# Third context attention: row maxima head by head on the whole TensorE array, its steps interleaved, and two of its four projections ahead of the feed-forward block

## The chip, the cores and the metric

The kernel runs on one core of one Trainium2 chip. The metric is the device time of one execution in microseconds; the text gives it as the median of three runs. TensorE's work appears in the profile under PE (the matmuls) and PEld (the loads of the stationary operand); DVE is VectorE, ACT is ScalarE, POOL is GpSimd and SP issues most DMAs.

## The reference

The program is a network of twelve residual blocks on `x` (4 batches of 128 tokens with 128 channels) with a context of 4 x 2048 rows of 96 values. The change concerns the tenth block, a cross-attention of 8 heads with 16 values each, and by its place the ninth, a feed-forward block with quantized weights. The tenth block, cut to what matters:

```
def _L3_xattn_ref(x, y, Wq, bq, Wk, bk, Wv, bv, Wo, bo):      # x: 4x128x128, y: 4x2048x96
    q, k, v = x @ Wq + bq, y @ Wk + bk, y @ Wv + bv           # 8 heads of 16
...
    weight = jnp.einsum('bhqd,bhkd->bhqk', q, k) * scale
    weight = jax.nn.softmax(weight, axis=-1)                  # over 2048 keys
    out = jnp.einsum('bhqk,bhkd->bhqd', weight, v)
    return out.transpose(0, 2, 1, 3).reshape(B, SQ, D_EMBED) @ Wo + bo
```

The block's input is the layer norm of `x`, and its result is added to `x`. All of it is in 32-bit floating point.

## The kernel before, in words

`program` (line 1847) runs the blocks one after another; each block's function opens its own pools of SBUF and PSUM, and a block's weights are loaded into two alternating buffers by `nxt()` of the block before (the list WEIGHTS, line 1839). Within a block the framework's scheduler may exchange instructions that do not depend on each other, so the order in the code is nearly, but not wholly, the order on an engine.

The ninth block, `bit_ffn` (from line 1678), is a chain on VectorE: two layer norms, a quantization to 8 bits, a small product on TensorE (`h_ps`, line 1738), a Gelu, a third layer norm over 512 columns, a second quantization and a second product (`y_ps`, line 1754). Ahead of that chain TensorE forms a sum over the weights (`tot`, line 1696), from which VectorE derives the weights' scale (`wm`, `wi`) and quantizes them (`qw`, lines 1704 to 1707).

The tenth block is `narrow_attention` (from line 553). Its heads are laid in two sets `s` of four; head `g` of a set lies in partitions 32g to 32g + 31, 16 of them its values, one a row of ones in the keys that carries a bias. After the layer norm the queries of all batches are formed (`q_ps`, line 582). Then come, for each batch `b`:

- `project(b)` (line 598) forms the keys `kT` (8 matmuls of 512 columns, `k_ps`, line 605) and the values `v` (16 matmuls of 136 columns, `v_ps`, line 616) and copies them to SBUF, the copies alternating between ScalarE and VectorE (`self.copy`, lines 318 and 320).
- `maxima(b, s, kT)` (line 625) forms all scores of a set with the queries in the rows (`s_ps`, line 633). The four heads use 32 rows of the array each, so four matmuls of 512 columns run side by side; they write two tiles of two PSUM banks each, and VectorE reduces each tile of 1024 columns to two maxima (`na_m`, line 638). At the end the smallest negated maximum of each head (`nmx`, line 641) is transposed (`m_tr`) and added to the queries (line 645), as the factor of the keys' row of ones.
- `weighted(b, s, ...)` (line 649) takes the keys in four groups of four chunks. For a group it forms the scores with the keys in the rows (`t_ps`, line 657, four heads side by side again), ScalarE takes exponentials (`p`, line 663), and one group later TensorE multiplies with the values (`av`, line 670).
- `finish` (line 679) divides by the sums and multiplies with the output weights (`o_tr`, `on_tr`, `y`).

The loop (lines 705 to 727) first projects batch 0 and takes its first maxima alone. Then a step is one group of `weighted` with one step of the maxima of the next set beside it, and one step of the projection of the next batch as long as there are any. Two PSUM banks stand for each `t_ps`, `s_ps`, `k_ps` and `v_ps` tile: all draw on one pool of three such tiles.

Of the kernel before, what the change touches and what calls it, by code (L numbers as in the profile page):

```python
# [9 lines left out]
F32 = mybir.dt.float32  # L10
# [4 lines left out]
ALU = mybir.AluOpType  # L15
AX = mybir.AxisListType.X
PSUM = bass.MemoryType.PSUM

P = 128
B = 4  # L20
# [250 lines left out]
class Net:  # L271
# [279 lines left out]


    def narrow_attention(self, nxt):

# [3 lines left out]


        nc, tc = self.nc, self.tc  # L560
        wqo, wkv = self.load("qo3"), self.load("kv3")
        scale = 1.0 / math.sqrt(ND)
        with ExitStack() as es:
            one = es.enter_context(tc.tile_pool(name="na1", bufs=1))
            wk = es.enter_context(tc.tile_pool(name="na2", bufs=2))
            pp = es.enter_context(tc.tile_pool(name="na3", bufs=4))
            ps = es.enter_context(tc.tile_pool(name="na_sc", bufs=3, space=PSUM))
            mi = es.enter_context(tc.tile_pool(name="na_mi", bufs=1, space=PSUM))
# [9 lines left out]

            q = one.tile([P, 2, N], F32, name="q")
            mm = ps.tile([P, 2, 512], F32, tag="sc", name="q_ps")  # L580
            for s in range(2):
                nc.tensor.matmul(mm[:, s], wqo[:, s * P : s * P + P], xT, start=True, stop=True)
                nc.vector.tensor_scalar(
                    q[:, s], mm[:, s], self.col("bq3")[:, s : s + 1], scale, ALU.add, ALU.mult)

            nmx = []
# [10 lines left out]

            def project(b):

                kT = wk.tile([P, 2, S], F32, tag="kT", name="kT")  # L600
                v = wk.tile([P, NCH, NH * VW], F32, tag="v", name="v")
                for at in range(0, S, 512):
                    mm = ps.tile([P, 2, 512], F32, tag="sc", name="k_ps")
                    for s in range(2):
                        nc.tensor.matmul(
                            mm[:, s], wkv[:, s * P : s * P + P],
                            self.ctxT[: DC + 1, b * S + at : b * S + at + 512], start=True, stop=True)
                    self.copy(kT[:, :, at : at + 512], mm)
                    yield kT, v
                for c in range(0, NCH, 6):  # L610
                    mm = ps.tile([P, 2, 512], F32, tag="sc", name="v_ps")
                    n = min(6, NCH - c)
                    for j in range(n):
                        at = b * S + (c + j) * P
                        w = NH * VW
                        nc.tensor.matmul(
                            mm[:, j // 3, j % 3 * w : j % 3 * w + w], self.ctxT[: DC + 1, at : at + P],
                            wkv[:, 2 * P : 2 * P + w], start=True, stop=True)
                    for j in range(0, n, 3):
                        k = min(3, n - j)  # L620
                        self.copy(
                            v[:, c + j : c + j + k].rearrange("p c w -> p (c w)"), mm[:, j // 3, : k * w])
                    yield kT, v

            def maxima(b, s, kT):

                qs = q[:, s, b * T : b * T + T]
                part = self.small(16, "na_m")
                for j in range(4):
                    ts = [ps.tile([P, 2, 512], F32, tag="sc", name="s_ps") for _ in range(2)]  # L630
                    for g in (0, 2, 1, 3):
                        lo = g * 32
                        nc.tensor.matmul(  # L633
                            ts[g // 2][:, g % 2], qs[lo : lo + 32], kT[lo : lo + 32, s, j * 512 : j * 512 + 512],
                            start=True, stop=True)
                    for i, t in enumerate(ts):
                        at = j * 4 + i * 2
                        nc.vector.tensor_reduce(part[:, at : at + 2], t, axis=AX, op=ALU.max, negate=True)  # L638
                    yield
                t = nmx[s]  # L640
                nc.vector.tensor_reduce(
                    t[:, ND::32], part.rearrange("p (j g) -> p g j", g=4), axis=AX, op=ALU.min)
                tr = mi.tile([P, B, P], F32, tag="mi", name="m_tr")
                nc.tensor.transpose(tr[:, 0], t, self.ident)
                nc.vector.tensor_add(qs, qs, tr[:, 0])
# [3 lines left out]
            def weighted(b, s, kT, v, av):  # L649

                qs = q[:, s, b * T : b * T + T]
                for c0 in range(0, NCH, 4):
# [13 lines left out]
                    def values(c0=c0, p=p):  # L666
                        for j in range(4):
                            for g in range(4):
# [3 lines left out]
                                    p[g // 2][:, g % 2, j], start=c0 + j == 0, stop=c0 + j == NCH - 1)  # L672

                    while late:
                        late.pop()()
# [23 lines left out]
            def run(*gens):  # L699

                gens = [iter(g) for g in gens if g is not None]
                while gens:
                    gens = [g for g in gens if next(g, gens) is not gens]

            for kv in project(0):
                pass
            run(maxima(0, 0, kv[0]))
            done = None
            for b in range(B):
                av = avp.tile([P, 2, P], F32, tag="av", name="av")  # L710
                more = iter(project(b + 1)) if b + 1 < B else iter(())
                ahead = []
                for s in range(2):
                    if s == 0:
                        top = maxima(b, 1, kv[0])
                    else:
                        top = maxima(b + 1, 0, ahead[0]) if ahead else None
                    for i, _ in enumerate(weighted(b, s, *kv, av)):
                        if done and i == 0:
                            finish(*done)  # L720
                            done = None
                        if top:
                            next(top)
                        ahead = next(more, ahead)
                    run(top)
                done = (b, av)
                kv = ahead
# [950 lines left out]
    def bit_ffn(self, nxt):  # L1678
# [3 lines left out]
        with ExitStack() as es:  # L1682
# [26 lines left out]
            def quantized(x, d, j):  # L1709
# [6 lines left out]
                nc.vector.tensor_scalar_mul(sc, sc, 127.0)  # L1716
                t = one.tile([P, B, d], F32, tag=f"qt{j}", name="qt")
                nc.vector.tensor_mul(t, x, bc_in(sc, d))
# [22 lines left out]
            nc.scalar.activation(self.flat(h), self.flat(h), AF.Gelu)  # L1741
            hn = one.tile([P, B, 512], F32, name="hn")
            self.layernorm(one, h, hn, w=self.row("ln2_g"), b=self.row("ln2_b"), tag="ln2")
            q, sc = quantized(hn, 512, 1)
            qT2 = one.tile([P, B, 4, P], BF16, name="qT2")
# [76 lines left out]
class _Doubled:  # L1822
# [17 lines left out]
    ("l0x",), ("mamba", "dtp"), ("l0f",), ("qk1", "vo1"), ("r7", "r7b"), ("moe1", "moe2"),  # L1840
    ("qk2", "vo2"), ("l2a",), ("l2f",), ("qo3", "kv3"), ("l3a",), ("l3f",),
]
# [4 lines left out]
def program(tc, A, out):  # L1847
    with ExitStack() as es:
        net = Net(es, tc, A)
        for i, (block, args) in enumerate(BLOCKS):  # L1850
# [9 lines left out]
            if i in CTX_TO:  # L1860
                ces.close()
        tc.nc.sync.dma_start(out.rearrange("b t c -> t b c"), net.x)

# [16 lines left out]
```

## Time and profile before

| | us |
|---|---|
| median of three runs | 1784.24 (1782.26 to 1784.53) |
| the profiled execution | 1783.64, span of its instructions 1781.5 |
| TensorE busy, PE (PEld) | 1273.4 (681.7) |
| VectorE, ScalarE, GpSimd busy | 1002.5, 631.2, 139.3 |
| mean granted TensorE clock | 0.801 |

The profile is of one execution, and its times are counted from the first instruction. A row of groups has the source line, the engine, the operation, the tiles written and read, the shapes and a count, then the busy time in us and the mean of one in ns, then the engine's idle time just before these instructions and what ended most of it. A 32-bit matmul appears as two rows of MATMUL and two of LDWEIGHTS, so counts of rows are twice the matmuls'. [...] successive ones overlap in the record, and the distance between their starts is the better price. A timeline row has the start, the time from the first start to the last end of the merged instructions, and in brackets the idle time before. In a table of stretches, each row has the stretch and its length, the busy time of the engines with the number of instructions, then the mean granted clock (1.00 is full speed), the DMA share and GB/s.

### The profile page before, as it was taken

To read this page: it belongs to the slowest core of one execution; us is meant where nothing else is said; L and a number is where in the kernel's file an instruction comes from. 1 tells how busy PE (TensorE), PEld (TensorE's weight loads), DVE (VectorE), ACT (ScalarE), POOL (GpSimd) and SP (SyncE) were. 2 spreads that over 40 slices of the span, in tenths; PEclk is the share of its full clock that TensorE was granted. 3 is DMA by queue.
4 is the path that set the end of the run, shared out by engine and by line. 5 is a ranking of instruction groups with operands and counts; after the bars stand their busy time and mean duration, and the time that the engine had idled before them with its cause. 6 is when DMAs were issued, how large, how long until landed. Compare 5 with 4: busy or idle time off the path is not lost.

```text
span 1781.5 us, 15501 instructions
## 1 busy us (share of the span) xinstructions
PE 1273.4 (71%) x6140; PEld 681.7 (38%) x6140; DVE 1002.5 (56%) x1556; ACT 631.2 (35%) x804; POOL 139.3 (8%) x107
## 2 busy tenths in 40 slices
PE   0367654667689999999946443889866518899867
PEld 0146641222343444444412222664324304554544
DVE  5842345999425676767656875223446674443435
ACT  0642114554315465656434101323422211333342
POOL 2000000446200000000000100000003010000000
PEclk9975555779858999999967766887878656998878
DMA  5000000000400000000001002100000000000010
GB/s 148 0 1 0 1 0 0 0 24 1 134 16 24 1 0 1 1 0 1 1 0 47 0 1 82 37 21 18 0 1 1 8 0 0 2 1 1 6 45 6
DMA packets 9076, 28.18 MB, mean 16 GB/s; under 512 B 1140, under 2 KB 6941, under 8 KB 7717
## 3 DMA queue, kind: packets, MB, share of 16 engines
q1 hardware_dynamic: 7208, 23.70, 4.6%
q10 hardware_dynamic: 1792, 3.45, 0.6%
q8 instruction: 50, 0.82, 0.2%
q14 instruction: 26, 0.21, 0.0%
HBM read 26.88 MB, written 0.26 MB: 15 GB/s over the span
## 4 chain that ended last, share of the span: by engine, by line
PE 62%; DVE 24%; ACT 5%; issue 5%; POOL 3%; DMA 1%; POOLq 0%; ACTq 0%; DVEq 0%
PE av L513 12%; PE sc L487 11%; PE av L933 3%; PE s_ps L633 3%; DVE na_m L638 3%; PE mm L1227 3%; PE t_ps L657 3%; PE q_ps L433 2%; DVE h L1144 2%; PE av L670 2%; PE h_ps L1576 2%; PE st L910 2%; PE y_ps L1583 2%; PE y_ps L1149 1%; POOL hc L1147 1%
## 5 line engine op out<-in xcount | busy, mean ns | idle before, releaser
L513 PE MATMUL av<-s,ctx 128*97 128x512 f32 x448 | 211.0, 629 | 19.4 <-ACT s L511 19.3
L487 PE MATMUL sc<-q_aug,ctxT 99*128 99x512 f32 x448 | 207.5, 607 | 1.8 <-DVE q_aug L434 1.8
L489 ACT COPY s<-sc 128x1024 f32<-128x1024 f32 x112 | 113.0, 1010 | 94.9 <-PE sc L487 94.9
L513 PEld LDWEIGHTS av<-s,ctx 128*97 128x97 f32 x448 | 76.6, 174 | 146.9 <-issue 108.9
L510 DVE TENSOR_TENSOR s<-s,mbs 128x1024 f32<-128x1024 f32 x112 | 128.9, 1219 | 5.0 <-ACT mbs L507 5.0
L638 DVE TENSOR_REDUCE na_m<-s_ps 128x2 f32<-128x1024 f32 x64 | 75.8, 1220 | 90.1 <-PE s_ps L633 89.9
L487 PEld LDWEIGHTS sc<-q_aug,ctxT 99*128 99x128 f32 x448 | 83.7, 195 | 96.3 <-issue 79.0
L511 ACT ACTIVATE s<-s 128x1024 f32<-128x1024 f32 x112 | 113.5, 1053 | 10.8 <-DVE s L510 8.2
L493 DVE TENSOR_TENSOR m<-m,s 128x1024 f32<-128x1024 f32 x72 | 88.0, 1223 | 21.9 <-ACT s L489 20.8
L1149 PE MATMUL y_ps<-hc,consts 128*128 128x512 f32 x128 | 75.1, 722 | 33.7 <-POOL hc L1147 30.8
L663 ACT ACTIVATE p<-t_ps 128x1024 f32<-128x1024 f32 x64 | 62.0, 1021 | 92.8 <-PE t_ps L657 92.8
L1147 POOL TENSOR_TENSOR hc<-h,cs 128x1024 f32<-128x1024 f32 x32 | 77.5, 2432 | 86.1 <-DVE h L1144 85.9
L524 DVE RECIPROCAL rsum<-y 128x2 f32<-128x2 f32 x40 | 6.6, 165 | 133.5 <-PE y L521 133.5
L1144 DVE TENSOR_TENSOR_SCAN h<-dA,dbu 128x512 f32<-128x512 f32 x64 | 74.4, 1204 | 3.7 <-ACT dA L1141 3.5
L933 PE MATMUL av<-kv,p 128*128 128x65 f32 x256 | 56.9, 419 | 19.1 <-ACT p L929 19.1
L336 POOL TENSOR_TENSOR ln_sq<-ln_xc 128x512 f32<-128x512 f32 (+1 forms) x19 | 23.3, 1225 | 552.7 <-DVE ln_xc L334 546.2
L633 PE MATMUL s_ps<-kT,q 32*128 32x512 f32 x256 | 63.5, 709 | 2.1 <-DVE na_m L638 1.1
L933 PEld LDWEIGHTS av<-kv,p 128*128 128x128 f32 x256 | 55.3, 332 | 21.0 <-ACT p L929 15.0
L657 PE MATMUL t_ps<-q,kT 32*128 32x128 f32 x1024 | 56.3, 328 | 8.8 <-DVE na_m L638 5.8
L353 PE MATMUL tr_xnT<-consts,xn 128*128 128x128 f32 x32 | 8.7, 428 | 70.3 <-DVE xn L343 30.2
L1149 PEld LDWEIGHTS y_ps<-hc,consts 128*128 128x128 f32 x128 | 26.0, 223 | 83.2 <-POOL hc L1147 57.0
L657 PEld LDWEIGHTS t_ps<-q,kT 32*128 32x128 f32 x1024 | 46.6, 223 | 27.1 <-DVE na_m L638 16.2
(574 smaller groups left out, 2122.0 us busy)
## 6 DMA issues: line engine op xcount, KB each, us to landing
w_moe<-in_moe SPq DMA_DIRECT2D x2, 2048.0 KB, 8.0
ctxT<-in_ctxT SPq DMA_DIRECT2D x4, 768.0 KB, 12.3
rows<-in_rows ACTq DMA_DIRECT2D x1, 2048.0 KB, 12.1
w_l3f<-in_l3f SPq DMA_DIRECT2D x1, 1920.0 KB, 8.2
w_l0x<-in_l0x SPq DMA_DIRECT2D x1, 1024.0 KB, 5.7
w_l0f<-in_l0f SPq DMA_DIRECT2D x1, 1024.0 KB, 4.9
w_mamba<-in_mamba SPq DMA_DIRECT2D x1, 976.0 KB, 4.7
w_r<-in_r SPq DMA_DIRECT2D x1, 960.0 KB, 5.1
```

Source lines behind the costliest of these rows:

```text
L487: nc.tensor.matmul(sc[:, i], self.ctxT[:, at : at + P], qg, start=True, stop=True)
L489: nc.scalar.copy(s, sc)
L510: nc.vector.tensor_sub(p, p, bc_mid(mbs, 2))
L511: nc.scalar.activation(p, p, AF.Exp)
L513: nc.tensor.matmul(av[: DC + 1], self.ctx[:, b * NCH + chunks[j + i]], p[:, i], start=j + i == 0, stop=j + i == n - 1)
L633: nc.tensor.matmul(ts[g // 2][:, g % 2], qs[lo : lo + 32], kT[lo : lo + 32, s, j * 512 : j * 512 + 512], start=True, stop=True)
L638: nc.vector.tensor_reduce(part[:, at : at + 2], t, axis=AX, op=ALU.max, negate=True)
L657: nc.tensor.matmul(ts[g // 2][:, g % 2, j], kT[g * 32 : g * 32 + 32, s, at : at + P], qs[g * 32 : g * 32 + 32], start=True, stop=True)
L933: nc.tensor.matmul(av[:, 0:65], ts[h][:, c], v[:, b * NCH + 2 * c + h], start=h + c == 0, stop=h == 1 and c == HC - 1)
L1144: nc.vector.tensor_tensor_scan(h[:, half], self.flat(dA), dbu[:, half], 0.0, ALU.mult, ALU.add)
L1147: nc.gpsimd.tensor_mul(hc, h, bc_mid(cs, 2))
L1149: nc.tensor.matmul(y[:, half], self.ident, hc[:, half], start=n == 0, stop=n == 15)
```

## The change

Five edits, all in or around the tenth block:

- A new function `narrow_keys` runs after the eighth block and before `bit_ffn`. It loads the weights of keys and values into a pool of its own and runs the projections of batches 0 and 1; `project` is now a method, works in tiles of one PSUM bank (14 a batch), and has all its copies on ScalarE.
- The queries are also laid out as `qz`: for each set and head a full 128 rows, zero outside of the head's 32. GpSimd writes the zeroes, ScalarE and VectorE copy the heads in.
- `maxima` forms the scores of one head at a time with `qz` on all 128 rows, into tiles of one bank from a pool of two (`sp`), and VectorE reduces each tile of 512 columns on its own. `t_ps` has a pool of two tiles of two banks instead of its share in three. The projections of batches 2 and 3 stay in the loop and draw on `sp` too, all in the first half of the batch before.
- A step of the loop is spread: two head steps of the maxima, the scores of a group, one head step, a projection tile, the product with the values of the group before, one head step, further projection tiles.
- In `bit_ffn` the third layer norm is taken in place, and one temporary shares a buffer.

In the built program the order on TensorE is: `out_ps` of the eighth block, the 48 matmuls of `narrow_keys`, then `tot` and the rest of `bit_ffn`. Within the loop a step without projections reads three `s_ps`, 16 `t_ps`, one `s_ps`, 16 `av`. On VectorE `wm`, `wi` and the quantization of the weights stand after the first quantization of the input instead of before the first layer norm. On GpSimd the zeroing of `qz` stands between the last square of `bit_ffn` and that of this block's layer norm.

```diff
+    def narrow_keys(self, es):
+        pool = es.enter_context(self.tc.tile_pool(name="na_w", bufs=1))
+        self.wkv = pool.tile(list(self.A["kv3"].shape), F32, name="w_kv3")
+        self.nc.sync.dma_start(self.wkv, self.A["kv3"])
+        self.kvp = es.enter_context(self.tc.tile_pool(name="na_kv", bufs=2))
+        self.kv = {}
+        with self.tc.tile_pool(name="na_kvps", bufs=3, space=PSUM) as ps:
+            for b in range(2):
+                for self.kv[b] in self.project(ps, b, self.nc.scalar.copy):
+                    pass
+    def project(self, ps, b, copy):
...
+        for at in range(0, S, 512):
+            for s in range(2):
+                mm = ps.tile([P, 512], F32, tag="s", name="k_ps")
...
+                copy(kT[:, s, at : at + 512], mm)
+                yield kT, v
+        for c in range(0, NCH, 3):
+            mm = ps.tile([P, 512], F32, tag="s", name="v_ps")
...
+            copy(v[:, c : c + n].rearrange("p c w -> p (c w)"), mm[:, : n * w])
+            yield kT, v
...
-            ps = es.enter_context(tc.tile_pool(name="na_sc", bufs=3, space=PSUM))
+            ps = es.enter_context(tc.tile_pool(name="na_sc", bufs=2, space=PSUM))
+            sp = es.enter_context(tc.tile_pool(name="na_s", bufs=2, space=PSUM))
...
+            qz = one.tile([P, 2, 4, N], F32, name="qz")
+            nc.gpsimd.memset(qz, 0.0)
...
+            for s in range(2):
+                for g in range(4):
+                    self.copy(qz[g * 32 : g * 32 + 32, s, g], q[g * 32 : g * 32 + 32, s])
...
-                    ts = [ps.tile([P, 2, 512], F32, tag="sc", name="s_ps") for _ in range(2)]
-                    for g in (0, 2, 1, 3):
-                        lo = g * 32
+                    for g in range(4):
+                        t = sp.tile([P, 512], F32, tag="s", name="s_ps")
                         nc.tensor.matmul(
-                            ts[g // 2][:, g % 2], qs[lo : lo + 32], kT[lo : lo + 32, s, j * 512 : j * 512 + 512],
+                            t, qz[:, s, g, b * T : b * T + T], kT[:, s, j * 512 : j * 512 + 512],
                             start=True, stop=True)
-                    for i, t in enumerate(ts):
-                        at = j * 4 + i * 2
-                        nc.vector.tensor_reduce(part[:, at : at + 2], t, axis=AX, op=ALU.max, negate=True)
-                    yield
+                        at = j * 4 + g
+                        nc.vector.tensor_reduce(part[:, at : at + 1], t, axis=AX, op=ALU.max, negate=True)
+                        yield
...
-                    for i, _ in enumerate(weighted(b, s, *kv, av)):
-                        if done and i == 0:
+                    steps = weighted(b, s, *kv, av)
+                    for i in range(NCH // 4):
+                        take(top, 2)
+                        next(steps)
+                        take(top, 1)
+                        ahead = next(more, ahead)
+                        next(steps)
+                        if done:
                             finish(*done)
                             done = None
-                        if top:
-                            next(top)
+                        take(top, 1)
                         ahead = next(more, ahead)
-                    run(top)
+                        if s == 0:
+                            ahead = next(more, ahead)
+                            ahead = next(more, ahead)
+                    take(top, 1)
...
-            hn = one.tile([P, B, 512], F32, name="hn")
-            self.layernorm(one, h, hn, w=self.row("ln2_g"), b=self.row("ln2_b"), tag="ln2")
-            q, sc = quantized(hn, 512, 1)
+            self.layernorm(one, h, h, w=self.row("ln2_g"), b=self.row("ln2_b"), tag="ln2")
+            q, sc = quantized(h, 512, 1)
```

`take(g, n)` calls `next` on a generator up to n times; in `weighted` a second `yield` now stands between the exponentials and the product with the values.

## The prediction

> **What bounds the kernel now.** I read the page's groups first, to see what the changed block costs; then the busy time by stretch, to cut the block into stages; then the timeline of one step, to see which wait ends last in it. The program is one long chain of blocks, so what counts is this block's length (1466.6 to 1717.1 us) and that of the feed-forward block ahead of it. From the page:
>
> ```profile
> L638 DVE TENSOR_REDUCE na_m<-s_ps 128x2 f32<-128x1024 f32 x64 | 75.8, 1220 | 90.1 <-PE s_ps L633 89.9
> L663 ACT ACTIVATE p<-t_ps 128x1024 f32<-128x1024 f32 x64 | 62.0, 1021 | 92.8 <-PE t_ps L657 92.8
> L633 PE MATMUL s_ps<-kT,q 32*128 32x512 f32 x256 | 63.5, 709 | 2.1 <-DVE na_m L638 1.1 <-ACT p L663 1.0
> ```
>
> VectorE and ScalarE sit idle for TensorE (89.9 and 92.8 us); TensorE's groups hardly wait. By stretch (us; busy PE, PEld, DVE, ACT, POOL; then the granted clock):
>
> ```profile
> 1410.60:1428.40 17.80, 1.19 (x6) 0.84 (x6) 13.62 (x33) 0.59 (x2) 2.08 (x2) 0.50 0.06 20
> 1428.40:1466.60 38.20, 5.96 (x36) 3.71 (x36) 27.33 (x30) 4.77 (x4) 4.45 (x5) 0.50 0.00 0
> 1466.60:1490.10 23.50, 16.56 (x56) 9.39 (x56) 9.94 (x15) 3.32 (x5) 1.54 (x1) 0.70 0.00 0
> 1490.10:1503.50 13.40, 9.19 (x35) 2.78 (x33) 10.54 (x12) 1.78 (x2) 0.00 (x0) 0.79 0.00 1
> 1503.50:1556.80 53.30, 48.65 (x626) 29.29 (x626) 23.83 (x26) 19.75 (x23) 0.00 (x0) 0.89 0.01 2
> ...
> 1610.50:1668.90 58.40, 53.81 (x631) 31.14 (x631) 24.97 (x31) 20.01 (x24) 0.00 (x0) 0.85 0.02 5
> 1668.90:1698.80 29.90, 25.25 (x294) 15.67 (x294) 11.11 (x14) 8.02 (x9) 0.00 (x0) 0.72 0.01 2
> ```
>
> In the feed-forward block (two first lines) TensorE is nearly unused and VectorE is the chain. In the loop over batches (from 1503.5) TensorE is busy nine tenths of the time. One step at full clock:
>
> ```profile
> 1578.87 0.98 PEld L657 LDWEIGHTS t_ps<-q,kT 32*128 32x128 f32 x30 [0.31 <-DVE na_m L638]
> 1579.97 1.07 PE L670 MATMUL av<-p,v 128*17 128x128 f32 x32
> 1580.14 1.94 ACT L663 ACTIVATE p<-t_ps 128x1024 f32<-128x1024 f32 x2 [0.76 <-PE t_ps L657]
> 1580.97 1.38 PE L633 MATMUL s_ps<-kT,q 32*128 32x512 f32 x8
> 1582.28 1.98 PE L605 MATMUL k_ps<-ctxT,w_kv 97*128 97x512 f32 x4
> 1582.39 2.36 DVE L638 TENSOR_REDUCE na_m<-s_ps 128x2 f32<-128x1024 f32 x2 [3.57 <-PE s_ps L633]
> 1584.20 0.28 PE L670 MATMUL av<-p,v 128*17 128x128 f32 x1
> ```
>
> Starts, not lengths, give the costs: t_ps 1.10 us (to 1579.97), av 1.00, the four packed heads of s_ps 1.31, two k_ps 1.92; with some 0.6 us of waiting a step of 5.93. The last price is from the timeline of TensorE alone, where one form runs unbroken:
>
> ```profile
> 1476.49 3.62 PE L605 MATMUL k_ps<-ctxT,w_kv 97*128 97x512 f32 x4
> 1481.19 5.32 PE L605 MATMUL k_ps<-ctxT,w_kv 97*128 97x512 f32 x12
> 1486.35 3.87 PE L616 MATMUL v_ps<-w_kv,ctxT 97*128 97x136 f32 x32
> ```
>
> Each matmul has two rows. At full clock 12 rows take 5.16 us (1481.19 to 1486.35), so 0.43 a row and **0.86 us a 512-column matmul**; ahead of 1480.8 it is 0.85 a row, the half clock. A batch's projection is 16 x 0.43 + 3.8 (1486.35 to 1490.1) = 10.7 us.
>
> [...] here the packed four take 1.31 us where four whole-array ones would take 3.44, 2.6 times, its switch included. [...] the pair of k_ps between two packed groups takes 1.92 us where 4 rows are 1.72, **0.2 us a phase**. [...] here it rose at 1480.8, 6 us after TensorE took up work at 1474.6[...]. [...]
>
> **The change, part by part.**
>
> *Maxima on the whole array.* 128 matmuls of 128x512 replace 128 packed ones that ran four at a time. In a step of the new order (three s_ps, t_ps, one s_ps, av) the phases are 6 x 0.43 + 0.2 = 2.78; 1.10; 0.86 + 0.2 = 1.06; 1.00. The two single banks add a wait: the third s_ps needs the first one's reduction. No 512-column na_m exists, but the reduction mq (line 502) from the same size of PSUM takes 0.69 us; a tile is 0.1 for weights + 0.86 + 0.16 for the drain, then 0.04 + 0.69 + 0.05, so the third starts 1.90 us after the first instead of 1.82, and loads its weights uncovered (0.1): 0.19. Behind that wait stands t_ps, and ScalarE's exponentials behind it, with slack. A step is **6.12 us** (5.2 if switches and waits were free, 6.6 if they were half as long again). Four reductions (2.8 us) and two exponentials (1.94) hide under it. Against before: 6.12 where a step had k or v work too and took 5.93; so the interleaving removes the waits, and the longer matmuls eat it.
>
> *Ends of a half.* The interleaving hides most of the m_tr chain: 0.25 us of TensorE remains. Half: 4 x 6.12 + 0.25 = 24.7; seven of them have maxima beside them: 173.1.
>
> *First maxima, alone.* Two banks let a tile out each 1.90 / 2 = 0.95 us: 15 x 0.95 + 2.4 for some 5 us at half clock = 16.7 (13.4 before).
>
> *Projections left in the loop* (batches 2 and 3; their copies now all on ScalarE): 10.7 + 14 tiles x 0.1 of bank wait + 0.9 behind exponentials = 13.0 each, 26.0. Bounds 10.7 and 18.
>
> *Finishing* three batches inside the loop: o_tr, on_tr and y, 1.2 each, 3.6. *Last half*, without maxima: 2.8 for the bare chain reduction, m_tr, q; then t_ps has one pair of buffers instead of three tiles, so each step is t_ps 1.1 + two exponentials 1.94 + hand-over 0.15 = 3.2; four, and half a microsecond for a clock that may fall: 13.5 (before 12.5 from 1698.85 to the last exponential's end). Tail as before, 5.7 (1711.4 to 1717.1).
>
> Sum from the first s_ps: 16.7 + 173.1 + 26.0 + 3.6 + 2.8 + 13.5 + 5.7 = **241.4**, where before took 1717.1 - 1490.1 = 227.0: **+14.4 us**.
>
> *Projections 0 and 1 ahead of the feed-forward block.* In the built order all 48 of their matmuls stand on TensorE between out_ps and tot, so tot, q_tr and h_ps queue behind them; w_kv goes into memory that alibi's queries left at 1392, so its load (2.3 us for the like w_qo) is in time. They can start at 1410.6, after out_ps is read. 2 x 10.7 + 2.8 for 5.5 us at half clock + 0.8 (ScalarE's first ln_sd and its table load stand among the copies, three banks deep) gives 1435.6. Then the last copy and tot, 0.7; wm, wi and the quantization of the weights, which in the new order follow q and no longer hide earlier, 2.7; qT 0.4: h_ps at 1439.5 instead of 1428.45, **+11.1** (9.5 to 13). VectorE's chain to q ends at about 1429 and waits. Against this stands what leaves the stage before the first s_ps: there 16 k_ps rows and v_ps fill 1476 to 1490. Without them s_ps follows q: q_ps read at 1476.74, 0.75 for q, about 1.1 for qz's copies, two on each of ScalarE and VectorE: 1478.6, **-11.5**.
>
> *qz's zeroes.* POOL's memset rows give 204 ns for 128 columns and 311 for 256, 0.84 ns a column, so 3.5 us for 4096; it starts where nmx's did (1465.6) and stands ahead of ln_sq (1469.0 before): +0.45. Below nothing it can't go; were POOL twice as slow it would cost 4.
>
> *Weights.* On SP w_kv now stands ahead of w_qo, but is free to go 18 us before w_qo is (1409.9); w_l3a loads earlier, w_l3f at the same place (after the last y), both with slack: nothing. Layer norm in place and the shared buffer of qt: the same instructions in VectorE's order: nothing.
>
> Total: 14.4 + 11.1 - 11.5 + 0.45 = **+14.5**. The profiled execution took 1783.64 (span 1781.5 and 2.1 around it), so 1798.1; the median of before lies 0.6 higher: **1798.7**.
>
> **Rivals.**
> *Faster: the switches vanish.* If the whole-array matmuls and their neighbours flowed with no drain, uncovered weights or bank wait, a step is 3.44 + 0.88 + 0.87 = 5.2 and 28 of them save 26: 1773. It decides from 5.6 us a step. For it: t_ps, av and s_ps follow one another with little visible gap[...]. Against: the 0.2 us at each side of k_ps is in every step.
> *Even.* Steps of 5.6 to 5.8 with copies never behind exponentials: 1784 to 1789.
> *Much slower: the clock.* Before has about 60 us of half clock in the loop (twice one minus the clock, times each stretch). My sum gives the new loop none after its start[...]. Were it the same 60 us, 30 more: 1828. For it: the clock fell to half in spells in every stretch shown; against: the pauses that I see there (0.6 us a step, 2 us at a half's end) go.
> *That it doesn't do what it says* is excluded by the built order.
>
> **How the numbers follow.** Main case 0.72 (1789 to 1812), even 0.08, faster 0.12, clock 0.08. The range, 1784 to 1815, leaves out the faster case and the clock case. A measurement of this kernel tells 0.2% (3.6 us) from no change: faster 0.12, same 0.06, slower 0.82.
>
> **What would show it.** h_ps starting near 1439.5; first s_ps near 1490; s_ps rows 0.43 apart, steps of 6.1 without projections and about 9 with them; clock near 1 from the second step on; the block's end near 1731. A step under 5.6, or h_ps under 1432, makes the sum wrong.

## The result, and the profile after

| | before | after |
|---|---|---|
| median of twelve runs, us | 1783.72 (1777.27 to 1786.43) | 1798.22 (1788.46 to 1807.02) |
| ratio to before, 95% interval | | 1.0086 [1.0067, 1.0106] |
| the profiled execution, us | 1783.64 | 1807.02 |
| mean granted TensorE clock | 0.801 | 0.815 |

The change costs 0.86%, about 15 us; 1798.7 was predicted. The profiled execution of after is the slowest of its twelve. It was 10.2 us late already at the end of the eighth block, in work that the change does not touch, and in the profiles of the kernels below that point lies anywhere between 1402 and 1420 us. Times of the two blocks are therefore counted from the addition of `out_ps` to `x`, which ends the eighth block (at 1409.9 in before, 1420.1 in after). The first `s_ps` is the start of its first weight load, and the end of the tenth block the start of the last addition of `y` to `x`:

| us after the eighth block | before | after | difference |
|---|---|---|---|
| first `h_ps` | 18.6 | 33.5 | +15.0 |
| first `y_ps` added to `x` | 55.5 | 69.2 | +13.6 |
| first `s_ps` | 80.2 | 83.2 | +3.0 |
| first `t_ps` | 93.6 | 104.9 | +11.3 |
| end of the tenth block | 306.9 | 321.0 | +14.1 |

The difference arises in these two blocks: 14.1 us here, 15 in the medians. The groups on the page of after that answer to the three of before:

```profile
L654 DVE TENSOR_REDUCE na_m<-s_ps 128x1 f32<-128x512 f32 x128 | 88.5, 692 | 108.3 <-PE s_ps L650 107.6
L650 PE MATMUL s_ps<-kT,qz 128*128 128x512 f32 x256 | 133.1, 634 | 0.0
L679 ACT ACTIVATE p<-t_ps 128x1024 f32<-128x1024 f32 x64 | 62.0, 1021 | 116.3 <-PE t_ps L673 116.3
```

The busy time of `s_ps` doubled, from 63.5 to 133.1 us, and the idle time of VectorE and ScalarE ahead of their parts rose by some 20 us each: both wait for TensorE more than before. By stretch (length; busy PE, PEld, DVE, ACT, POOL; then the granted clock, the DMA share and GB/s):

```profile
1420.80:1453.60 32.80, 24.26 (x102) 14.69 (x102) 13.97 (x33) 17.26 (x32) 2.08 (x2) 0.86 0.05 14
...
1503.30:1525.00 21.70, 21.70 (x45) 7.29 (x44) 15.10 (x24) 2.78 (x4) 0.00 (x0) 0.89 0.00 0
1525.00:1575.50 50.50, 50.50 (x612) 26.01 (x612) 22.79 (x36) 17.31 (x19) 0.00 (x0) 1.00 0.01 2
...
1700.00:1741.40 41.40, 35.40 (x514) 21.62 (x513) 12.06 (x25) 16.36 (x20) 0.00 (x0) 0.94 0.01 2
```

From the first maxima (1503.3) up to the last half TensorE is busy nearly without a gap, and from 1508 on its clock is full, where before the loop had a clock of 0.72 to 0.89. The first line is the stretch up to `h_ps`: 32.8 us long, of which TensorE works 24.3. One step of the loop on TensorE:

```profile
1531.16 3.04 PE L650 MATMUL s_ps<-kT,qz 128*128 128x512 f32 x6
1534.13 1.17 PE L673 MATMUL t_ps<-q,kT 32*128 32x128 f32 x32
1535.23 1.12 PE L650 MATMUL s_ps<-kT,qz 128*128 128x512 f32 x2
1536.29 1.07 PE L686 MATMUL av<-p,v 128*17 128x128 f32 x32
1537.29 3.03 PE L650 MATMUL s_ps<-kT,qz 128*128 128x512 f32 x6
```

From start to start it takes 6.13 us; the four parts are 2.97, 1.10, 1.06 and 1.00. TensorE's rows at the head of after show what the 32.8 us hold:

```profile
1417.97 2.07 PE L1697 MATMUL out_ps<-w_l2a,oT 128*128 128x128 f32 x8 [0.68 <-ACT oT L318]
1425.85 7.19 PE L574 MATMUL k_ps<-ctxT,w_kv 97*128 97x512 f32 x12 [5.80 <-DMA w_kv<-in_kv]
...
1450.20 0.38 PE L1726 MATMUL tot<-bf_s,ones 128*128 128x2 f32 x2 [0.53 <-ACT v L588]
1450.44 0.38 PE L1762 MATMUL q_tr<-identb,q 128*128 128x128 bf16 x4
1453.63 1.03 PE L1768 MATMUL h_ps<-qw,qT 128*128 128x512 bf16 x2 [2.81 <-DVE qT L1764]
```

The bracket of `k_ps` is the finding: TensorE stood idle for 5.8 us for the weights of keys and values.

### The profile page after: what moved, and what is told of

Read it like the earlier page. It is cut to its first block, busy times and chain, and to the rows that moved or that the text cites. A ratio compares the mean times of both kernels' runs of the same rounds, so it can differ in the third digit from the quotient of the medians.

```text
span 1805.2 us, 15601 instructions
## 1 busy us (share of the span) xinstructions
PE 1327.5 (74%) x6140; PEld 695.8 (39%) x6140; DVE 1003.4 (56%) x1604; ACT 647.7 (36%) x844; POOL 143.0 (8%) x108
## 4 chain that ended last, share of the span: by engine, by line
PE 65%; DVE 21%; ACT 5%; issue 5%; POOL 2%; DMA 2%; POOLq 0%; ACTq 0%; DVEq 0%; SPq 0%
PE av L513 12%; PE sc L487 11%; PE s_ps L650 7%; PE av L963 3%; PE mm L1257 3%; DVE h L1174 2%; PE q_ps L433 2%; PE t_ps L673 2%; PE av L686 2%; PE h_ps L1606 2%; PE st L940 2%; PE y_ps L1613 2%; PE k_ps L574 1%; PE y_ps L1179 1%; POOL hc L1177 1%
## 5 line engine op out<-in xcount | busy, mean ns | idle before, releaser
L654 DVE TENSOR_REDUCE na_m<-s_ps 128x1 f32<-128x512 f32 x128 | 88.5, 692 | 108.3 <-PE s_ps L650 107.6
L489 ACT COPY s<-sc 128x1024 f32<-128x1024 f32 x112 | 113.0, 1010 | 93.6 <-PE sc L487 93.6
L650 PE MATMUL s_ps<-kT,qz 128*128 128x512 f32 x256 | 133.1, 634 | 0.0
L487 PEld LDWEIGHTS sc<-q_aug,ctxT 99*128 99x128 f32 x448 | 83.2, 194 | 95.5 <-issue 77.7
L963 PEld LDWEIGHTS av<-kv,p 128*128 128x128 f32 x256 | 55.3, 332 | 21.0 <-ACT p L959 15.0
L650 PEld LDWEIGHTS s_ps<-kT,qz 128*128 128x128 f32 x256 | 41.1, 192 | 52.5 <-DVE na_m L654 29.0
L1171 ACT ACTIVATE dA<-delta,A 128x508 f32<-128x508 f32 x64 | 42.6, 689 | 33.2 <-DVE h L1174 32.3
```

The costliest lines, as they stand in the source:

```text
L487: nc.tensor.matmul(sc[:, i], self.ctxT[:, at : at + P], qg, start=True, stop=True)
L489: nc.scalar.copy(s, sc)
L650: nc.tensor.matmul(t, qz[:, s, g, b * T : b * T + T], kT[:, s, j * 512 : j * 512 + 512], start=True, stop=True)
L654: nc.vector.tensor_reduce(part[:, at : at + 1], t, axis=AX, op=ALU.max, negate=True)
L963: nc.tensor.matmul(av[:, 0:65], ts[h][:, c], v[:, b * NCH + 2 * c + h], start=h + c == 0, stop=h == 1 and c == HC - 1)
```

## The experiments

All kernels at a glance. "Gap" has both projections behind `h_ps`, "lead" the maxima one step ahead, "spread" the finishing of a batch over four steps; unless "whole array" or "after" is said, the attention is the packed one of before. "Over before" is the ratio less one, times the median of before. "End of block" is the end of the tenth block, counted as above, less that of before (306.9); the last column is the time at half clock (in us) between the first `t_ps` and that end, added up from the trace's clock records.

| kernel | median, us | ratio to before, 95% | over before, us | first `s_ps` | end of block | half clock |
|---|---|---|---|---|---|---|
| before | 1783.72 | | | 80.2 | | 59.7 |
| after | 1798.22 | 1.0086 [1.0067, 1.0106] | +15.3 | 83.2 | +14.1 | 4.4 |
| projections moved only | 1784.31 | 1.0009 [0.9992, 1.0026] | +1.6 | 84.4 | +0.1 | 63.4 |
| whole array only | 1802.63 | 1.0120 [1.0093, 1.0148] | +21.4 | 78.9 | +23.1 | 6.8 |
| after, early load | 1791.51 | 1.0051 [1.0034, 1.0067] | +9.1 | 78.5 | +9.5 | 6.8 |
| after, load split | 1791.08 | 1.0049 [1.0034, 1.0065] | +8.7 | 78.6 | +9.5 | 6.8 |
| after, three banks | 1801.30 | 1.0114 [1.0083, 1.0144] | +20.3 | 83.1 | +19.2 | 16.3 |
| after, four in a row | 1787.77 | 1.0043 [1.0029, 1.0058] | +7.7 | 83.2 | +6.2 | 0.0 |
| gap | 1777.27 | 0.9967 [0.9954, 0.9980] | -5.9 | 71.6 | -6.6 | 80.7 |
| lead | 1779.77 | 0.9982 [0.9967, 0.9996] | -3.2 | 80.2 | -2.7 | 55.7 |
| gap, lead | 1759.79 | 0.9885 [0.9855, 0.9915] | -20.5 | 71.6 | -19.6 | 49.3 |
| lead, spread | 1761.25 | 0.9894 [0.9868, 0.9920] | -18.9 | 80.2 | -18.8 | 32.7 |
| gap, lead, spread | 1746.97 | 0.9803 [0.9777, 0.9829] | -35.1 | 71.6 | -32.9 | 32.7 |
| gap, whole array, four in a row | 1777.63 | 0.9974 [0.9957, 0.9990] | -4.6 | 71.6 | -5.7 | 1.6 |

The ends of the block give the same order as the medians, within 2.2 us.

### Which half of the change costs

My theory was that the whole-array maxima cost and the move of the projections gains; the rival, that the move costs. The first kernel has before's attention and after's `narrow_keys`:

```diff
-        wqo, wkv = self.load("qo3"), self.load("kv3")
+        wqo, wkv = self.load("qo3"), self.wkv
-            for kv in project(0):
-                pass
+            kv = self.kv[0]
-                more = iter(project(b + 1)) if b + 1 < B else iter(())
-                ahead = []
+                ahead = self.kv.get(b + 1)
+                more = iter(()) if ahead or b + 1 == B else iter(project(b + 1))
```

> The attention of before (packed maxima, two reductions of 1024 columns a step, the old loop), with projections 0 and 1 ahead of the feed-forward block as in after. Theory (the longer matmuls of the whole array cost, the move gains): h_ps starts 15 us later against the end of the block ahead than before, as it did in after, the first s_ps only 1 to 3 us later, because the 16 k_ps rows and v_ps that stood there are gone; the loop's eight steps of batch 0 lose 1.9 us of k or v work each and some wait, 8 to 12 us in all, unless the clock falls in the pauses that this opens. Sum about 8 us under before: near 1775 (1768 to 1783). Rival (the move is what made after slower, since it delays h_ps by 15 us): 1790 or more.

Neither came: the ratio has no change in its interval. `h_ps` came 16.5 us later, the first `s_ps` 4.2 us (84.4 against 80.2), as expected but for 1 us. The first maxima then took 15.9 us instead of 13.4, at a granted clock of 0.50 throughout, and batch 0 from its first `t_ps` to its end 51.2 us instead of 57.7. A projection less is 10.7 us by the price in the prediction, so 4 of them are missing: in that stretch TensorE's time without work rose from 4.7 us (57.70 less 53.02 busy) to 9.3 (51.30 less 41.99), and its granted clock fell from 0.90 to 0.85. So the move is neither gain nor loss with the packed attention: what it saves in batch 0, 6.5 us, goes to the later first `s_ps` (4.2) and to the first maxima at half clock (2.5).

The second has the maxima and steps of after and projects batch 0 at its old place and in its old banks:

```diff
-        with self.tc.tile_pool(name="na_kvps", bufs=3, space=PSUM) as ps:
-            for b in range(2):
-                for self.kv[b] in self.project(ps, b, self.nc.scalar.copy):
-                    pass
...
-            kv = self.kv[0]
+            for kv in self.project(Old(), 0, self.copy):
+                pass
```

> The whole-array maxima and the interleaved steps of after, with no projection ahead: batch 0 is projected at its old place behind q_ps, batch 1 in the loop. Theory: h_ps as in before; the loop has three projections instead of two, some 12 us more than after's 238.1 us from the first s_ps to the end of the block, so 24 us over before: near 1807 (1801 to 1813). Rival (whole-array maxima cost nothing, the move does): at or under before, 1784 or less.

1802.63, with the end of the block at +23.1 where 24 was expected: the theory holds. The whole-array maxima with their steps cost some 22 us, and the move gives 6 to 9 of them back.

### The load that was late

Two kernels test the 5.8 us in the bracket of `k_ps`. One loads the weights ahead of the eighth block:

```diff
+            if block == "alibi_attention":
+                nes = es.enter_context(ExitStack())
+                pool = nes.enter_context(tc.tile_pool(name="na_w", bufs=1))
+                net.wkv = pool.tile(list(A["kv3"].shape), F32, name="w_kv3")
+                tc.nc.sync.dma_start(net.wkv, A["kv3"])
             getattr(net, block)(*args, nxt)
```

> After, with the weights of keys and values loaded ahead of the eighth block instead of behind it, so that they are in SBUF when k_ps could start. Theory (TensorE's wait for that load, 5.8 us ahead of k_ps, stands on the path to h_ps): k_ps starts within 0.6 us of out_ps being read, h_ps and the end of the block come 5 us earlier: near 1793 (1791 to 1795.5). Rival (VectorE's own chain to the first quantization sets h_ps, the wait is hidden): no change, 1798.

The other leaves the load where it is and cuts it in two:

```diff
-        self.nc.sync.dma_start(self.wkv, self.A["kv3"])
+        for lo, hi in ((0, 96), (96, 97)):
+            self.nc.sync.dma_start(self.wkv[lo:hi], self.A["kv3"][lo:hi])
```

> After, with the load of the 97 rows of the key and value weights cut into one of 96 rows and one of a single row, issued one after the other at the same place. Theory[...]: the pair lands 2.5 to 3.5 us after its issue instead of 8.4, k_ps starts with out_ps read, h_ps and the end of the block come 5 us earlier, as with the early load: near 1792 (1790 to 1795). Rival (8.4 us is what a load takes at that place, behind other traffic): no change, 1798.

Both land at 1791, 6 to 7 us under after, and both end the block 4.6 us earlier. The list of DMA issues of the second (transfer, count, KB, us to landing) and TensorE's rows:

```profile
w_kv<-in_kv SPq DMA_DIRECT2D x1, 147.0 KB, 2.2
```

```profile
1408.83 2.07 PE L1698 MATMUL out_ps<-w_l2a,oT 128*128 128x128 f32 x8 [0.67 <-ACT oT L318]
1411.69 8.03 PE L575 MATMUL k_ps<-ctxT,w_kv 97*128 97x512 f32 x12 [0.78 <-DVE x L1699]
```

In after the load is issued at 1417.37, just ahead of the last product of the eighth block; the last increment of its semaphore comes 8.3 us later (1425.71), and releases `k_ps`. With 96 rows nearly the same bytes land in 2.2 us, and `k_ps` waits only 0.78 us, for `out_ps` to be read: one row fewer made the load nearly four times as fast. The packets in the traces show how: those of the 97 rows run one after another, at most two at a time, from 1418.27 to 1425.28, where those of the 96 rows and the single one run up to 19 at a time, from 1409.18 to 1410.03. In before the 128 packets of w_qo, one a row, also run up to 19 at a time, from 1410.84 to 1411.92. The 97 packets of this load run just as slowly there, from 1413.95 to 1421.07, which rules out the rival of other traffic at the new place. What sets the number at a time was not shown.

### The price of a step

A step was priced with 0.19 us for a wait on a bank and 0.2 us for each of its changes between the whole and the split array (1.92 us less 1.72 for the pair of `k_ps` in before). With three banks:

```diff
-            sp = es.enter_context(tc.tile_pool(name="na_s", bufs=2, space=PSUM))
-            mi = es.enter_context(tc.tile_pool(name="na_mi", bufs=1, space=PSUM))
+            sp = es.enter_context(tc.tile_pool(name="na_s", bufs=3, space=PSUM))
+            mi = sp
```

> After, with three single banks for the maxima instead of two (the small transposes draw on the same three). Theory: the third s_ps of a step no longer waits for the first one's reduction; 0.19 us in each of 28 steps is 5.3, and the first maxima, which let a tile out each 0.95 us with two banks, come 1 to 2 us sooner: near 1791.5 (1789 to 1794). Rival (the wait is hidden or moves to the exponentials): no change, 1798.

The step is 5.93 us, 0.19 shorter, as priced, and the first maxima take 19.8 us instead of 21.7. The kernel is slower all the same. In the batches with projections the steps between two `t_ps` reach 15.0 and 16.7 us (9.6 in after); there the finishing transposes share the three banks with `s_ps` and `k_ps`, and in batch 3 the clock falls for 6.8 us just after TensorE has waited 0.6 us ahead of `o_tr`. That the shared banks cause it is argued, not tested alone. With four head steps in a row:

```diff
-                        take(top, 2)
-                        next(steps)
-                        take(top, 1)
+                        take(top, 4)
+                        next(steps)
                         ahead = next(more, ahead)
                         next(steps)
-                        take(top, 1)
```

> After, with the four head steps of the maxima in a row in each step of the loop (order 4 s_ps, 16 t_ps, 16 av) instead of 3 and 1. Theory: one pair of changes between whole and split array fewer saves 0.2 us a step, but the fourth s_ps now waits for a bank as the third does, 0.1 to 0.2: a step of 5.95 to 6.1, 1 to 5 us in all: near 1795 (1793 to 1798). Rival (changes of mode cost nothing, what I priced there is waits for banks): steps of 6.2 or more, 1800 or more.

```profile
1545.82 1.17 PE L673 MATMUL t_ps<-q,kT 32*128 32x128 f32 x32
1546.93 1.07 PE L686 MATMUL av<-p,v 128*17 128x128 f32 x32
1547.92 3.89 PE L650 MATMUL s_ps<-kT,qz 128*128 128x512 f32 x8
1551.75 1.17 PE L673 MATMUL t_ps<-q,kT 32*128 32x128 f32 x32
```

A step is 5.93 us (1545.82 to 1551.75): one pair of changes less saves 0.2 us, and the rival is out. The kernel is 7.7 us under after by the ratios and 7.9 by the end of the block, more than 28 steps give (5.6): batch 3 takes 33.0 us instead of 36.9 from the end of batch 2.

### The gap of the feed-forward block

In the 38.2 us of before that hold `h_ps` and `y_ps` TensorE works 5.96. This kernel has before's packed attention, the early load, and both projections behind `h_ps`, in the banks of `h_ps`, which keeps the scheduler from taking them ahead:

```diff
             nc.scalar.activation(self.flat(h), self.flat(h), AF.Gelu)
+            for b in range(2):
+                for self.kv[b] in self.project(ps, b, nc.scalar.copy, "mm"):
+                    pass
```

> The packed attention of before with projections 0 and 1 put behind h_ps inside the feed-forward block, where TensorE was nearly idle for 30 us, and the weights loaded ahead of the eighth block. Theory: h_ps is not delayed, the projections (25 us at the half clock) end before y_ps needs TensorE, the first s_ps comes 11.5 us earlier than in before, and the steps of batch 0 lose 8 to 12 us: near 1763 (1756 to 1772). Rival (the copies on ScalarE or the shared PSUM banks hold up the feed-forward block's own chain, or the clock eats it): 1780 or more.

Faster than before, but by less than a third of what was expected. The head does nearly its part: `h_ps` at 19.0, the first `s_ps` 8.6 us earlier. But batch 0 takes 57.2 us from its first `t_ps`, as long as with a projection in it (57.7), at a granted clock of 0.74 instead of 0.90, and with 9 us without work on TensorE instead of 4.7. Where TensorE had less to do, its clock was lower.

The same place with after's attention and four head steps in a row:

> After with four head steps in a row, the weights of keys and values loaded ahead of the eighth block, and projections 0 and 1 behind h_ps instead of ahead of it. Theory: the head gains 11 us against after (the first s_ps at 72 us past the end of the eighth block's product instead of 83), the steps 8, and the first maxima lose up to 5 because the clock is not up there yet: near 1781 (1777 to 1785), level with before, without half clock in the loop. Rival (after's clock in the loop depends on the projections just ahead of it): the loop shows spells of half clock, 1788 or more.

1777.63, at the lower end of what was expected, and with 1.6 us of half clock: the loop of after keeps its clock without projections just ahead of it, and the rival is out.

### What brings the clock down

Why does the packed loop fall to half clock (59.7 us of it in before) and the other hardly (4.4 in after)? Before waits at the end of every batch for the reduction, `m_tr` and the sum with `q` (at the end of a batch's first half the wait for `m_tr` is only 0.4 to 0.5 us):

```profile
1552.95 1.07 PE L670 MATMUL av<-p,v 128*17 128x128 f32 x32
1556.13 0.33 PE L644 MATMUL m_tr<-consts,nmx 128*128 128x128 f32 x1 [2.11 <-DVE nmx L641]
1556.84 1.17 PE L657 MATMUL t_ps<-q,kT 32*128 32x128 f32 x32 [0.38 <-DVE q L645]
1557.94 0.44 PE L685 MATMUL o_tr<-consts,o 128*128 128x128 f32 x2
```

The next kernel hides it, and does nothing else: a set's maxima run one step ahead, so that the chain falls into a half's last step.

```diff
-                    yield
+                    if j < 3:
+                        yield
...
                 nc.vector.tensor_add(qs, qs, tr[:, 0])
+                yield
...
-            run(maxima(0, 0, kv[0]))
+            kvs = {0: kv}
+            def tops():
+                for b in range(B):
+                    for s in range(2):
+                        yield from maxima(b, s, kvs[b][0])
+            top = tops()
+            for _ in range(5):
+                next(top)
```

> Before (packed maxima, nothing moved ahead), with the maxima of each half begun one step earlier, so that a half's last step has the first maxima of the half after next beside it and the chain of reduction, m_tr and q is hidden under it: of the change it keeps only the hiding of that chain. Theory: the granted clock is at half for 48 us of the loop of before, in spells that begin where TensorE pauses for that chain at the end of a half; without the pauses (some 2.5 us each, seven of them) and with most of those spells gone the loop is 20 to 30 us shorter: near 1760 (1750 to 1770). Rival[...]: only the pauses themselves are saved, some 10 us, and the spells of half clock stay: 1772 or more.

My theory failed: 3 us were saved, and 55.7 us of half clock remained. The rival had some 10 us for the pauses alone; TensorE's time without work in the loop fell by only 2.5 us (22.4 to 19.9), since other waits took their place. The trace shows what is late next. `o_tr` follows `t_ps` at once in before, since the copies of `av` were made while TensorE waited for `m_tr`. Here that wait is gone, and TensorE waits for the copies:

```profile
1564.13 1.38 PE L633 MATMUL s_ps<-kT,q 32*128 32x512 f32 x6
1566.93 0.41 PE L687 MATMUL o_tr<-consts,o 128*128 128x128 f32 x2 [1.42 <-DVE o L320]
1567.27 1.23 PE L633 MATMUL s_ps<-kT,q 32*128 32x512 f32 x2
```

The clock fell to half at 1568.2, at the end of these rows, for 10.2 us. The same in the kernel with the gap:

> The kernel with the projections in the gap of the feed-forward block, with the hidden chain of the run before it as well. Theory: what the earlier kernel with the gap lost was the clock in batch 0's steps (half of 63 us in them); if the hidden chain holds the clock up there too, 6.5 us of the head, 20 to 30 of the pauses and 10 of batch 0's projection work come together: near 1745 (1735 to 1757). Rival (steps without projection work leave TensorE idle for the exponentials and reductions, and the clock falls in batch 0 all the same): 6.5 under the kernel with the hidden chain alone, no more.

Here both edits together bring 20.5 us, more than the 5.9 and 3.2 that each brings alone. The cause of that surplus was not tested; the result lies between the two theories. The next pair removes the wait for the copies: copies, `o_tr`, `on_tr` and `y` of a finished batch each go into a step of their own.

```diff
             def finish(b, av):
                 o = os[b % 2]
                 for g in range(0, P, 32):
                     self.copy(o[g : g + VW], av[g : g + VW])
+                yield
...
-                        if done and i == 0:
-                            finish(*done)
-                            done = None
+                        next(fin, None)
```

> The kernel with the hidden chain alone (nothing moved ahead), with the finishing spread over four steps. Same theories: by the first, the three spells at the batches' starts go, 18 to 25 us less than that kernel: near 1759 (1754 to 1767). By the rival 4 to 5 us less: 1774 or more.

> The kernel with the gap and the hidden chain, with the finishing of a batch (copies, o_tr, on_tr, y) spread over the four steps of the next half instead of all in its first. Theory ([...] the wait for the copies ahead of o_tr, 1.4 us, is the one left at each batch's start): three spells of 10 to 14 us go, 5 to 7 us each, and the waits: 18 to 25 us less, near 1738 (1733 to 1746). Rival (the packed work as such lets the clock fall, wherever the waits lie): the waits alone, 4 to 5 us less, 1754 or more.

```profile
1561.00 1.07 PE L672 MATMUL av<-p,v 128*17 128x128 f32 x32
1562.00 0.44 PE L688 MATMUL o_tr<-consts,o 128*128 128x128 f32 x2
1562.37 1.14 PE L633 MATMUL s_ps<-kT,q 32*128 32x512 f32 x8
```

These rows are from the first of the two; `o_tr` waits for nothing. By the ends of the block it is 16.1 us faster than without the spread, and the second 13.3 (18 to 25 were expected of each, 4 to 5 by the rival). What the spread took away was waits of 1.42, 1.42 and 1.33 us ahead of `o_tr` and one of 1.12 ahead of `on_tr`, 5.3 us in all, by the traces of the kernels without it. But TensorE's time without work did not fall. From the first `t_ps` to the end of the block, with the lead alone and with the lead and the spread:

```profile
sum 209.30, PE 189.36 PEld 119.81 DVE 84.15 ACT 77.05 POOL 0.00; mean PE 47.34 PEld 29.95 DVE 21.04 ACT 19.26 POOL 0.00
sum 193.10, PE 173.31 PEld 111.96 DVE 84.43 ACT 76.81 POOL 0.00; mean PE 43.33 PEld 27.99 DVE 21.11 ACT 19.20 POOL 0.00
```

The length less PE's busy time is 19.9 us in the first and 19.8 in the second (24.8 and 24.2 in the pair with the gap). Waits ahead of `t_ps` grew instead, from 9.1 to 14.0 us; the longest stands where VectorE now copies `av` ahead of a reduction:

```profile
1658.47 1.87 PE L659 MATMUL t_ps<-q,kT 32*128 32x128 f32 x24 [2.09 <-DVE na_m L638]
```

So nearly all of the gain is TensorE's busy time, 16.0 us (12.8 in the pair with the gap). Half clock fell from 55.7 to 32.7 us there, and from 49.3 to 32.7 in the kernel with the gap; half of that, 11.5 and 8.3, is an estimate of its worth, since a row of `k_ps` in before took 0.85 us at half clock and 0.43 at full. Some 4.5 us of each pair are not placed. The spread also changed something else: without it `on_tr` and `y` cut a step's `t_ps` into three parts (1572.14 to 1576.72 in the kernel with the lead), and that was not tested alone. **In the packed loop, moving 5.3 us of waits away from the finishing was worth 13 to 16 us, most of it, by that estimate, as time at half clock, though TensorE stood idle as long as before.** With all three edits the packed kernel is 2.0% faster than before, the fastest of this study. Of its 32.7 us at half clock, 10.4 are the start of batch 0, the rest spells of 3.4 to 6.8 us.

What exactly brings the clock down was not found. In the first of the two a wait of 0.83 us ahead of `t_ps` (1600.8) brought no fall. In the traces of before and after each spell of half or full clock but the last, cut off by the end, lasts a multiple of 3.41 us (in the loop of before 6.83, 13.65, 17.07, 40.96 and 47.79); call 3.41 us a window. In before a window with 0.40 of busy time in the records came ahead of a fall (285.9 us past the eighth block) and one with 0.46 did not (142.5), but windows with 0.89 and 1.00 came ahead of falls too (84.5 and 149.4). So the busy share of the records does not decide it, and what does was not shown.

## Why the prediction was right

The predicted total, +14.5, met 14.1 at the end of the block and 15 in the medians. The terms did less well, and two errors of 3 to 4 us cancelled by luck.

- **The step.** Predicted 6.12, measured 6.12 and 6.13, with its parts right one by one: 1.06 for the single `s_ps` with its change, 0.19 for the wait on a bank (three banks: 5.93), 0.2 for a pair of changes (four in a row: 5.93). The 1.90 for a tile was an estimate from gaps in before: 0.1 from a weight load to its matmul (1383.58 and 1383.68), 0.16 by which the record of 12 rows (5.32) is longer than the way to the next start (5.16), 0.04 from a matmul's end to the reduction (1582.35 and 1582.39), 0.05 from a reduction's end to the weights (1578.82 and 1578.87).
- **The halves.** The five without projections take 22.7, 25.3, 25.1, 24.5 and 25.8 us, 123.4; predicted 5 x 24.7. The last of them has a finishing in it and is 0.8 longer than the mean of the three ahead of it. The two with projections take 36.8 each, 11.0 more than that one, where 13.0 was charged. That leaves 0.3 over the 10.7 of their matmuls for waits on banks and exponentials; the 1.4 and 0.9 charged for these were estimates.
- **First maxima.** Tiles leave in pairs each 1.91 us, as predicted (0.95 a tile). The stage up to the first `t_ps` took 21.7, not 16.7: 20 `s_ps` stand ahead of it instead of the 16 that I counted. Four tiles are 3.8 us, which the first half gives back in part. Of the other 1.2, 0.85 lie between the first weight load (1503.29) and the first matmul (1504.14), which queues behind `q_ps`. The 5 us at half clock were an estimate from before, whose clock rose to full at 1480.8, 6.1 us after `q_ps` began (1474.6); here it rose at 1508.0, 4.7 us after the first weight load.
- **Last half.** 1721.9 to 1741.4 is 19.5 us, where 2.8 + 13.5 + 5.7 = 22.0 was charged. The bare chain of `m_tr`, 2.8, does not stand there: it is hidden like the others.
- **Attention in sum.** 238.1 us from the first `s_ps` to the end, predicted 241.4; too high by 3.3.
- **h_ps, the step that failed.** It was put at +11.1, with w_kv "free to go 18 us before w_qo" and a load of 2.3 us "for the like w_qo". Both were wrong. The load was issued 2.7 us ahead of w_qo's, since by the trace it waited for the eighth block's last tiles (`o`, `tr_oT`), not only for its queries, and it took 8.3 us to land, where w_qo's 128 rows took 2.3 in before and the same 97 rows, cut into 96 and one, 2.2. With the load out of the way `h_ps` starts at 29.6 (early) and 29.3 us (split): +11.0 and +10.7, so the rest of that term stands. The 4 us too few here, of which 3 reach the first `s_ps`, and the 3.3 too many in the loop nearly cancel.
- **First s_ps.** Net of +11.1, -11.5 and +0.45 I had +0.05; it was +3.0. To the 3.9 of `h_ps` come two terms put at nothing or too low. From `h_ps` to the first `y_ps` added, after takes 1.4 us less: ScalarE's table load for the Gelu, 1.28 us, stands behind `h` in before (1432.04) and ahead of `h_ps` in after (1450.16). And the zeroing of `qz` delayed the layer norm by 0.9 us, not 0.45. With the load of the weights out of the way the first `s_ps` is 1.7 us earlier than before.
- **The clock.** After has 218.5 us of full clock without a break; the rival with 60 us of half clock did not happen. What I took as a condition was a main term; that the clock stays full where TensorE does not pause was my estimate. Compare with an estimate: 28 steps went from 4.01 us (5.93 less 1.92 for k work) to 6.12, +59; the first maxima +8.3; against it one projection less, -10.7, the seven waits at the ends of halves, 9.4 ahead of `m_tr` and 4 x 0.38 behind it, -10.9, and 55.3 us fewer at half clock, -27.6. The sum is +18.2; the attention took 11.1 longer, so some 7 us of gain are not placed. Whole-array maxima in this order of steps come with a full clock and a loop nearly without waits, and pay more than that for their longer matmuls. Whether the matmuls or the order keep the clock up was not taken apart.
- **The faster rival** needed 5.6 us a step. The best order tried reaches 5.93.
- **Two sums** do not come out of their own terms: four steps of 3.2 and 0.5 are 13.3, not 13.5, and 1465.6 + 3.5 is 0.1 past 1469.0, not 0.45. Neither matters for the total.

## What to carry to other kernels

Before paying for longer matmuls to be rid of waits and half clock, look for the short waits at the ends of the loop's phases: here hiding them in the packed loop gave 1.1% (2.0% with the projections in the gap), where the change lost 0.9%. When a wait is hidden, ask which copy was made in its shadow: here TensorE next waited for that, 1.42 us. Give a load that is moved the price of its own row count and of the moment its memory comes free, not the price of its neighbour in the list: here 97 rows took 8.3 us, 96 rows and one 2.2, and the neighbour's 128 rows 2.3.

## What the runs showed of the hardware that I had not expected

- 148.5 KB in 97 rows landed 8.3 us after issue; 147 KB in 96 rows in 2.2.
- TensorE's waits moved to another place, with the same sum (19.9 and 19.8 us), and its time at half clock fell from 55.7 to 32.7 us.
- Taking 10.7 us of matmuls out of a batch that kept TensorE busy for 92% of its time saved 0.5 us (57.7 to 57.2), in the kernel with the gap: its clock fell from 0.90 to 0.74.
- A small VectorE instruction of the layer norm (`ln_m`) beside GpSimd's memset of `qz` (3.51 us) took 1.10 us where it took 0.17 in before; it ended with the memset (1492.94 and 1492.92).
